# A GRU scan on one core: a quarter of the z product moved behind the turns of r*h, one filling unit moved behind the candidate in four steps of eight, and another order of three PSUM banks

## The chip, the core and the metric

The kernel runs on one core of one Trainium2 chip. The metric is the device time of one execution in microseconds. Three runs of the kernel before took 1352.71, 1353.44 and 1355.67 us; their median, 1353.44 us, is the time that the change is held against.

## The reference

A GRU runs over 128 steps for a batch of 64, with input and hidden width 512, all in float32. Every fourth step but the last also sends the new state through a dense layer with tanh, and that result is the state of the next step. The output is the input plus the states.

```python
def step(h, inp):
    x_t, prop = inp
    comb = jnp.concatenate([x_t, h], axis=-1)
    z = jax.nn.sigmoid(comb @ Wz + bz)
    r = jax.nn.sigmoid(comb @ Wr + br)
    comb2 = jnp.concatenate([x_t, r * h], axis=-1)
    h_cand = jnp.tanh(comb2 @ Wh + bh)
    h_new = (1.0 - z) * h + z * h_cand
    h_next = jnp.where(prop, jnp.tanh(h_new @ Wp + bp), h_new)
    return (h_next, h_new)
...
x = x + transpose(ys)
```

## The kernel before, in words

**Layout.** A state is a tile of 128 partitions and 256 columns: partitions 0 to 63 hold the batch with the first half of the hidden width, partitions 64 to 127 the batch with the second half. A matmul needs the state turned, so that the hidden width lies on the partitions. `turn` (line 206) does that for one half of the columns (c = 0 or 1): four bf16 transposes on TensorE, which move the float32 words as pairs of 16-bit words into PSUM, and one copy out of PSUM by VectorE or ScalarE (line 204), which joins the pairs.

**One product** of a gate is `h @ W` with the 512x512 lower half of a weight matrix: four quarters k of the contraction, each for the two halves of the output (`product`, line 197, and `products`, line 185). It appears in the profile as sixteen matmul records on line 188, so a quarter is four records. `ORDER` (line 201) takes both quarters that use column half c = 0 first, so that a product can start when half 0 of the turned state is there. The products of r and of the candidate go to the two halves of bank `rc`, those of z and of the dense layer to the two halves of bank `zp`. ScalarE seeds each slot beforehand with the x part and bias of that step (`seed`, line 393).

**The x parts** (`x @ W`, upper half of the weights) don't depend on the state. They are cut into small units that TensorE does between the products of the steps, where it would wait for the other engines. For the bulk of the steps the x parts of several steps are made with a scheme of seven products inside seven products, which saves multiplications and costs additions. `batch` (line 482) makes two of the outer products as fourteen units: two in bank `a`, then two each in banks `q`, `r` and `x` (`one_`, line 520), after which `end_1` (line 499) reads all four; then two each in `x`, `q`, `r` on top of what stands there (`two_`, line 521), after which `end_2` (line 511) reads `q` by ScalarE (line 514) and then `r`, `x`, `q` by VectorE (lines 515, 516 and 517, in this order). A unit is two logical matmuls and four records of 128x192.

**The order of the work** is written out by hand, engine by engine, in the order of the program text; each engine takes its own queue in order. `fill(n)` (line 401) issues the next n units. When a unit closes a batch half, its `end` isn't issued at once but at the next `read_out()` (line 411).

A step t (line 624 on) goes like this. TensorE: product r (line 660). ScalarE: two sigmoids of r (line 675); VectorE: two multiplications r*h (line 676). Meanwhile TensorE: product z, all four quarters (line 681). Then the two turns of r*h (line 685), copied by VectorE; then `fill(places[0])` (line 705); then the candidate's product (line 710), which needs the turned r*h. ScalarE has by then taken the sigmoid of z and of -z (lines 690 and 691), and VectorE `keep` = (1-z)*h (line 692). After the candidate: tanh on ScalarE (line 717), times z and plus `keep` on VectorE (lines 718 and 723), in two halves. TensorE meanwhile: `fill(5)` if `places[1]` is over 6, else `fill(4)` (line 727); turn of half 0 of the new state, copied by VectorE (line 731); `fill(1)` or `fill(2)` by the same rule (line 732); turn of half 1, copied by ScalarE (line 733); `fill(places[1] - 6)` (line 734). Then, in every fourth step, the dense layer's product, four units, its turns and two units (lines 740 to 751). Then the next step's product r.

`PLACES` (line 586) holds the counts for a cycle of eight steps, u = (t-3) mod 8. The last nine steps are called thin: they have their own table and already put half of the z product behind the turns of r*h, one quarter behind each turn.

Of the kernel before, what the change touches and what calls it, by code (L numbers as in the profile page):

```python
# [17 lines left out]
def kernel(  # L18
# [36 lines left out]
    K = D // P  # L55
# [4 lines left out]
    R, Z, H_ = range(3)  # L60
# [20 lines left out]
    wh = [const.tile([P, K, H], F32, name=f"wh_{i}") for i in range(3)]  # L81
# [49 lines left out]
    for g in (2, 3):  # L131
# [10 lines left out]
    slots = (rc[:, 0, :], zp[:, 0, :], rc[:, 1, :])  # L142
    slot_p = zp[:, 1, :]
    scratch = [ps_c.tile([P, 2 * N], F32, name=f"scratch_{n}") for n in "qrax"]
    q_ps, r_ps, a_ps, x_ps = (
        s[:, : 6 * P // 2].rearrange("p (m g u) -> p m g u", m=2, g=3) for s in scratch
    )
# [37 lines left out]
    def products(ps, lhs, rhs, start=False):  # L185

        for s in range(S):
            nc.tensor.matmul(  # L188
                ps[s * B : (s + 1) * B],
                lhsT=lhs,  # L190
                rhs=rhs(s),
                start=start,
                stop=True,
                skip_group_check=True,
            )

    def product(ps, lT, w, k, start=False):
        s0, c0 = divmod(k, C)
        products(ps, lT[:, c0, ts(s0, B)], lambda s: w[:, k, ts(s, N)], start)

    ORDER = [s * C + c for c in range(C) for s in range(S)]
# [4 lines left out]
    def turn(src, dst, c, name, eng):  # L206


        pt = turn_ps[c][:, :P].bitcast(BF16).rearrange("p (w n) -> p w n", w=2)
        for s in range(S):  # L210
            words = src[:, c * P + s * B : c * P + (s + 1) * B].bitcast(BF16)
            for w in range(2):
                nc.tensor.transpose(  # L213
                    pt[s * B : (s + 1) * B, w, :],
                    words.rearrange("p (n w) -> p w n", w=2)[:, w, :],
                    ident16,
                )
        copy(
            eng,
            dst[:, c, :].bitcast(U16).rearrange("p (n w) -> p n w", w=2),  # L220
            pt.bitcast(U16).rearrange("p w n -> p n w"),
        )

    def new_T(tag, name):
        return two.tile([P, C, P], F32, tag=tag, name=name)
# [71 lines left out]
    def factor(i, j):  # L297

        return {
            1: lambda: inner(i, 0, 0),  # L300
            2: lambda: inner(i, 1, 0),
            3: lambda: inner(i, 1, 1),
            4: lambda: tt[:, i - 1, 2],
            5: lambda: inner(i, 0, 1),
            6: lambda: tt[:, i - 1, 0],
            7: lambda: tt[:, i - 1, 1],
        }[j]()
# [57 lines left out]
    def lhs(g, i, j):  # L365

        if i in (1, 2):
            rows, s = (xT[g][:, 0, i - 1], xT[g][:, 1, i - 1]), lambda n: sx[g, 12][:, n, i - 1]
        elif i == 4:
            rows, s = (xT[g][:, 2, 1], xT[g][:, 3, 1]), lambda n: sx[g, 4][:, n]  # L370
        else:
            key, tab, n0 = {
                5: ("o12", 56, 0), 6: ("o12", 56, 1), 7: ("o34", 73, 0), 3: ("o34", 73, 1)
            }[i]
            o = sx[g, key][:, n0]
            rows, s = (o[:, 0], o[:, 1]), lambda n: sx[g, tab][:, n, n0]
        if j in (1, 2):
            return rows[0][:, ts(j - 1, B)]
        if j == 4:
            return rows[1][:, ts(1, B)]  # L380
        return s({5: 0, 6: 1, 7: 2, 3: 3}[j])
# [100 lines left out]
    def batch(n, ms):  # L482

        def region(ps, m):
            return ps[:, m].rearrange("p g u -> p (g u)")

        def unit(ps, m, j, start):
            g, i = ms[m]
            products(
                region(ps, m), lhs(g, i, j), lambda s: factor(i, j)[:, s], start and m == 0  # L490
            )

        def units(ps, j, start):
            return [lambda m=m: unit(ps, m, j, start) for m in range(len(ms))]

        def blocks():
            return MB[n].rearrange("p m b g (a u) -> p m b a g u", a=2)

        def end_1():
            MB[n] = mbp.tile([P, 2, 2, 3, P], F32, tag="mb", name=f"mb_{ms[0][0]}_{ms[0][1]}")  # L500
            for m, (g, i) in enumerate(ms):
                M[g, i] = MB[n][:, m]
            nm = len(ms)
            T2[n] = one.tile([P, 2, 3, P // 2], F32, tag="cx", name=f"cx_{ms[0][0]}_{ms[0][1]}")
            q1 = one.tile([P, 2, 3, P // 2], F32, tag="cq", name=f"cq_{ms[0][0]}_{ms[0][1]}")
            nc.scalar.copy(T2[n][:, :nm], x_ps[:, :nm])  # L506
            nc.scalar.copy(q1[:, :nm], q_ps[:, :nm])
            nc.vector.tensor_add(T2[n][:, :nm], r_ps[:, :nm], T2[n][:, :nm])  # L508
            nc.vector.tensor_add(blocks()[:, :nm, 0, 0], a_ps[:, :nm], q1[:, :nm])

        def end_2():
            q2 = one.tile([P, 2, 3, P // 2], F32, tag="cq", name=f"cq2_{ms[0][0]}_{ms[0][1]}")
            nm = len(ms)
            nc.scalar.copy(q2[:, :nm], q_ps[:, :nm])  # L514
            nc.vector.tensor_add(blocks()[:, :nm, 0, 1], r_ps[:, :nm], q2[:, :nm])  # L515
            nc.vector.tensor_add(blocks()[:, :nm, 1, 0], x_ps[:, :nm], q2[:, :nm])  # L516
            nc.vector.tensor_add(blocks()[:, :nm, 1, 1], q_ps[:, :nm], T2[n][:, :nm])  # L517

        free = units(a_ps, 2, True)
        one_ = units(q_ps, 1, True) + units(r_ps, 5, True) + units(x_ps, 7, True)  # L520
        two_ = units(x_ps, 4, False) + units(q_ps, 6, False) + units(r_ps, 3, False)
        seq = [(u, None) for u in free + one_ + two_]
        for n_units, end in ((4 * len(ms), end_1), (7 * len(ms), end_2)):
            seq[n_units - 1] = (seq[n_units - 1][0], end)
        return seq
# [4 lines left out]
    def batches(g):  # L530

        if g * Q4 >= T:
            return []
        ms = [(g, i) for i in (1, 2, 6, 5, 7, 3, 4)]
        if g + 1 < LAST:
            ms += [(g + 1, i) for i in (1, 6, 2, 5, 3, 7, 4)]
        return sum((batch((g, n), ms[2 * n : 2 * n + 2]) for n in range(7) if 2 * n < len(ms)), [])
# [43 lines left out]
    def outer_c21(g):  # L581
# [2 lines left out]


    PLACES = (
        (6, 8, 6), (2, 6), (6, 6), (2, 6), (6, 8, 6), (2, 6), (2, 6), (6, 8),
    )


# [14 lines left out]
    hT = new_T("hT", "hT_init")  # L605
# [18 lines left out]
    for t in range(T):  # L624
# [16 lines left out]
        thin = t >= T - 9  # L641
# [36 lines left out]
        join(0)  # L678


        for k in ORDER[: 2 if thin else K]:
            product(slots[Z], hT, wh[Z], k)
        rhT = new_T("rhT", f"rhT_{t}")
        for c in range(C):
            turn(rh, rhT, c, f"rhT_{t}", nc.vector)
            if thin:
                product(slots[Z], hT, wh[Z], ORDER[2 + c])
        z = two.tile([P, N], F32, tag="z", name=f"z_{t}")
        keep = two.tile([P, N], F32, tag="keep", name=f"keep_{t}")
        nc.scalar.activation(z, slots[Z], AF.Sigmoid)  # L690
# [38 lines left out]
        if not last:  # L729
            hT = new_T("hT", f"hT_{t}")  # L730
# [9 lines left out]
        if prop:  # L740
# [7 lines left out]
            hT = new_T("hT", f"hpT_{t}")  # L748
# [122 lines left out]
```

## Time and profile before

| what | value |
|---|---|
| median of three runs | 1353.44 us |
| the profiled execution: its time | 1353.16 us |
| its span, first to last instruction | 1351.3 us |
| what lies around the span | 1.9 us |
| TensorE matmuls busy | 1339.2 us, 15344 records |
| VectorE busy | 679.8 us |
| ScalarE busy | 628.2 us |
| GpSimd busy | 910.1 us |
| DMA traffic | 76.21 MB, 56 GB/s on average |
| TensorE clock granted | 0.997 of full speed |

How to read it: the span is that of one execution. "Busy" is the time in which an engine has at least one instruction under way. For matmuls the ends are modelled, so that a row of matmuls with small stalls between them can still show as busy without a break; the starts of instructions and the chain of work that ended last show more. In the timeline, equal instructions that follow each other are merged into one line, with their count; a bracket gives the idle time of the engine before it, and what is taken to have ended it. In the chain view, each line gives the start of a piece, its length and the engine and tile.

### The profile page before, as it was taken

The numbers are of one execution on the slowest core, as the hardware profiler recorded it, in microseconds if no ns is written. First come the engines' busy times: TensorE is split into PE (matmuls) and PEld (weight loads), VectorE is DVE, ScalarE is ACT, GpSimd is POOL, SyncE is SP. The second block draws the span as 40 slices with busy tenths as digits, with TensorE's granted clock in tenths as the row PEclk, the third lists the DMA queues.
The fourth block names the chain that finished last, engine by engine and source line by source line (L and its number), as shares of the span: only waits on it lengthen the run. The fifth ranks groups of instructions, "written<-read, shape, count | busy, mean of one in ns | idle before, by whom it ended". The sixth has DMA issues, their size and how long they took to land.

```text
span 1351.3 us, 37427 instructions
## 1 busy us (share of the span) xinstructions
PE 1339.2 (99%) x15344; PEld 1114.8 (82%) x15344; DVE 679.8 (50%) x1868; ACT 628.2 (46%) x1848; POOL 910.1 (67%) x1111
## 2 busy tenths in 40 slices
PE   9999999999999999999999999999999999999998
PEld 6878888888888888888888888888888888888765
DVE  3355555555555555554555555555555555555444
ACT  1234545444544544455445454545445444554433
POOL 3438676777767777676787767787677776767400
PEclk8999999999999999999999999999999999999999
DMA  9111223122321212313212231222213222131300
GB/s 280 22 33 33 64 48 79 33 49 48 64 64 33 64 42 55 64 33 73 52 35 64 56 73 33 49 48 64 64 33 64 48 49 64 33 73 39 102 17 17
DMA packets 114867, 76.21 MB, mean 56 GB/s; under 512 B 61700, under 2 KB 109956, under 8 KB 114696
## 3 DMA queue, kind: packets, MB, share of 16 engines
q1 hardware_dynamic: 113632, 72.04, 23.7%
q8 instruction: 121, 1.98, 0.6%
q10 hardware_dynamic: 1064, 1.78, 0.4%
q14 instruction: 50, 0.41, 0.1%
HBM read 42.34 MB, written 16.78 MB: 44 GB/s over the span
## 4 chain that ended last, share of the span: by engine, by line
PE 98%; DVE 1%; ACT 0%; issue 0%; POOL 0%; DVEq 0%; ACTq 0%; POOLq 0%
PE rc L188 34%; PE zp L188 20%; PE scratch_q L188 11%; PE scratch_x L188 11%; PE scratch_r L188 10%; PE scratch_a L188 6%; PE turn L213 5%; PE scratch_q L180 0%; PE zp L161 0%; ACT xT L204 0%; DVE rh L676 0%; PE rc L161 0%; DVE mb L516 0%; DVE mb L517 0%; DVE turn L718 0%
## 5 line engine op out<-in xcount | busy, mean ns | idle before, releaser
L188 PE MATMUL rc<-wh,rhT 128*64 128x256 f32 x2048 | 247.5, 381 | 0.0
L188 PEld LDWEIGHTS rc<-wh,rhT 128*64 128x64 f32 x2048 | 167.3, 137 | 45.2 <-ACT zp L691 9.3
L544 POOL TENSOR_TENSOR cp<-mb,mb 128x768 f32<-128x768 f32 x72 | 130.9, 1818 | 103.2 <-ACT rc L395 61.1
L188 PE MATMUL rc<-wh,hT 128*64 128x256 f32 x1536 | 186.6, 383 | 0.5
L188 PE MATMUL zp<-wh,hT 128*64 128x256 f32 x1536 | 186.9, 379 | 0.0
L803 POOL TENSOR_TENSOR xr<-xr,h 128x256 f32<-128x256 f32 x127 | 92.9, 732 | 115.2 <-DVE h L723 114.2
L204 DVE COPY rhT<-turn 128x256 uint16<-128x256 uint16 x256 | 97.6, 420 | 119.8 <-PE turn L213 118.8
L188 PEld LDWEIGHTS zp<-wh,hT 128*64 128x64 f32 x1536 | 130.4, 137 | 31.4
L718 DVE TENSOR_TENSOR turn<-turn,z 128x128 f32<-128x128 f32 x256 | 75.4, 295 | 148.9 <-ACT turn L717 148.8
L544 POOL TENSOR_TENSOR cp<-mb 128x768 f32<-128x768 f32 x44 | 80.0, 1818 | 103.6 <-ACT rc L395 102.4
L188 PEld LDWEIGHTS rc<-wh,hT 128*64 128x64 f32 x1536 | 123.0, 136 | 27.0 <-issue 1.3
L204 ACT COPY hT<-turn 128x256 uint16<-128x256 uint16 x127 | 47.3, 373 | 170.2 <-PE turn L213 113.6
L508 DVE TENSOR_TENSOR cx<-scratch_r,cx 128x384 f32<-128x384 f32 x102 | 56.7, 556 | 129.5 <-ACT cx L506 129.5
L675 ACT ACTIVATE turn<-rc 128x128 f32<-128x128 f32 x256 | 55.4, 261 | 141.3 <-issue 72.5
L717 ACT ACTIVATE turn<-rc 128x128 f32<-128x128 f32 x256 | 55.2, 260 | 131.5 <-PE rc L188 131.5
L544 POOL TENSOR_TENSOR mb<-mb,mb 128x768 f32<-128x768 f32 x58 | 105.7, 1822 | 12.5 <-DVE mb L517 12.5
L515 DVE TENSOR_TENSOR mb<-scratch_r,cq 128x384 f32<-128x384 f32 x102 | 56.7, 556 | 98.8 <-ACT cq L514 98.8
L395 ACT COPY rc<-cp 128x256 f32<-128x256 f32 x254 | 95.6, 376 | 13.2 <-PE rc L188 1.7
L274 ACT COPY xT<-xv 128x512 uint16<-128x512 uint16 x112 | 85.7, 765 | 0.0
L723 DVE TENSOR_TENSOR h<-turn,keep 128x128 f32<-128x128 f32 x254 | 74.1, 292 | 15.4
L690 ACT ACTIVATE z<-zp 128x256 f32<-128x256 f32 x128 | 49.2, 385 | 65.6 <-PE zp L188 60.8
L213 PEld LDWEIGHTS <-h 128*64 128x64 bf16 x1016 | 59.7, 110 | 22.2 <-DVE h L723 12.3
(156 smaller groups left out, 2981.2 us busy)
## 6 DMA issues: line engine op xcount, KB each, us to landing
xr<-in_x_dram SPq DMA_DIRECT2D x62, 256.0 KB, 4.2
out_dram<-xr SPq DMA_DIRECT2D x62, 256.0 KB, 3.4
xs<-in_x_dram SPq DMA_DIRECT2D x56, 256.0 KB, 4.2
wh<-in_L_cond_Wr_dram SPq DMA_DIRECT2D x2, 512.0 KB, 7.5
wh<-in_L_cond_Wz_dram SPq DMA_DIRECT2D x2, 512.0 KB, 6.6
wh<-in_L_cond_Wh_dram SPq DMA_DIRECT2D x2, 512.0 KB, 9.1
early<-in_x_dram SPq DMA_DIRECT2D x4, 256.0 KB, 12.2
wp<-in_L_cond_Wp_dram SPq DMA_DIRECT2D x1, 1024.0 KB
```

What stands on the lines that cost most here:

```text
L188: nc.tensor.matmul(ps[s * B : (s + 1) * B], lhsT=lhs, rhs=rhs(s), start=start, stop=True, skip_group_check=True,)
L204: (eng.copy if eng is nc.scalar else eng.tensor_copy)(dst, src)
L213: nc.tensor.transpose(pt[s * B : (s + 1) * B, w, :], words.rearrange("p (n w) -> p w n", w=2)[:, w, :], ident16,)
L274: nc.scalar.copy(xT[g][:, i].bitcast(U16).rearrange("p c (n w) -> p w c n", w=2), xv[g][:, i])
L395: nc.scalar.copy(cut(slots[i]), G[t][:, :, i, :])
L508: nc.vector.tensor_add(T2[n][:, :nm], r_ps[:, :nm], T2[n][:, :nm])
L515: nc.vector.tensor_add(blocks()[:, :nm, 0, 1], r_ps[:, :nm], q2[:, :nm])
L544: nc.gpsimd.tensor_add(dst, a, b)
L675: nc.scalar.activation(act_ps[c], slots[R][:, ts(c, P)], AF.Sigmoid)
L718: nc.vector.tensor_mul(pc, pc, z[:, ts(c, P)])
L723: nc.vector.tensor_add(h_new[:, ts(c, P)], pc, keep[:, ts(c, P)])
L803: nc.gpsimd.tensor_add(xr[g][:, j, :], xr[g][:, j, :], h_new)
```

## The change

Three things change, all in the order in which TensorE's instructions are issued; no instruction is added or taken away.

1. In all steps but the last nine, three quarters of the z product stand ahead of the turns of r*h, and the fourth follows both turns.
2. In the four steps of eight whose entry in `PLACES` was (2, 6), it is now (1, 7). By the rules of lines 705 and 727 to 734, one unit instead of two stands ahead of the candidate's product; behind it stand five units, the turn of half 0, one unit, the turn of half 1 and one unit, instead of four units, turn, two units, turn and none. The sum stays at eight units a step.
3. In the first half of a batch the banks are filled in the order r, x, q instead of q, r, x.

```diff
-        one_ = units(q_ps, 1, True) + units(r_ps, 5, True) + units(x_ps, 7, True)
+        one_ = units(r_ps, 5, True) + units(x_ps, 7, True) + units(q_ps, 1, True)
...
     PLACES = (
-        (6, 8, 6), (2, 6), (6, 6), (2, 6), (6, 8, 6), (2, 6), (2, 6), (6, 8),
+        (6, 8, 6), (1, 7), (6, 6), (1, 7), (6, 8, 6), (1, 7), (1, 7), (6, 8),
     )
...
-        for k in ORDER[: 2 if thin else K]:
+        for k in ORDER[: 2 if thin else 3]:
             product(slots[Z], hT, wh[Z], k)
         rhT = new_T("rhT", f"rhT_{t}")
         for c in range(C):
             turn(rh, rhT, c, f"rhT_{t}", nc.vector)
             if thin:
                 product(slots[Z], hT, wh[Z], ORDER[2 + c])
+        if not thin:
+            product(slots[Z], hT, wh[Z], ORDER[3])
         z = two.tile([P, N], F32, tag="z", name=f"z_{t}")
```

## The prediction

> **What bounds the kernel now.** I read the page first: TensorE's share of busy time, then the chain of work that ended last.
>
> ```profile
> PE 98%; DVE 1%; ACT 0%; issue 0%; POOL 0%; DVEq 0%; ACTq 0%; POOLq 0%
> ```
>
> The chain is TensorE almost throughout, and a table of windows gives 1062.00 us of matmul in the 1062 us from 118 to 1180: no idle time at all. That reading can't show small stalls, so I went to the chain in order of time, where each stage has its own length.
>
> ```profile
> 582.89 0.86 PE scratch_q L188 x8
> ...
> 607.65 1.79 PE rc L188 x16
> 609.44 0.65 PE scratch_q L188 x8
> 610.09 0.65 PE scratch_r L188 x8
> 610.74 0.15 PE turn L213 x4
> 610.89 0.65 PE scratch_x L188 x8
> 611.54 0.11 PE turn L213 x4
> 611.65 1.83 PE rc L188 x16
> 613.48 1.73 PE zp L188 x16
> ```
>
> Equal work takes unequal time. A product is 1.73 us (z, last line), but the candidate's took 1.79 and the r product of the next step 1.83; half a turn is 0.11, but one took 0.15; two units are 0.65, but those of bank q behind the dense layer took 0.86. The excess is stall. In this step, a (2, 6) one, it is 0.06 + 0.04 + 0.10 = 0.20 us. Steps with three units or more at each place have 1.73 and 0.11 throughout.
>
> Who is late is seen in the timeline (start, length, engine, line).
>
> ```profile
> 607.46 1.52 PEld L188 LDWEIGHTS rc<-wh,rhT 128*64 128x64 f32 x16 [0.16 <-ACT zp L691]
> ...
> 610.98 0.41 DVE L204 COPY hT<-turn 128x256 uint16<-128x256 uint16 x1
> ...
> 611.50 1.52 PEld L188 LDWEIGHTS rc<-wh,hT 128*64 128x64 f32 x16
> ```
>
> The weight load is named as waiting for ScalarE, but it needs the turned r*h: turns begin at 606.58, VectorE's first copy of them ends near 607.34. The r product of the next step waits in the same way: its copy ends at 611.39, its load starts 0.11 later, its first matmul at 611.54, 0.04 behind its load. The stall of bank q is VectorE's line 517:
>
> ```profile
> 582.28 0.55 DVE L517 TENSOR_TENSOR mb<-scratch_q,cx 128x384 f32<-128x384 f32 x1
> ...
> 582.88 0.20 PEld L188 LDWEIGHTS scratch_q<-tw,o 128*64 128x64 f32 x4 [0.44 <-DVE mb L517]
> ```
>
> **The Trainium skill.** "Perfetto Trace Analysis", section "Tensor Engine Instruction (MATMUL, LD_WEIGHTS)", says that a matmul's end is an estimate and its start is what is recorded; this trace agrees (busy without a break, yet 1.83 beside 1.73), so I use starts. "TensorE: Matmul & The Clock Gate", section "Step-by-step: what each phase is for", says that weight loads are pulled ahead of running matmuls while matmuls keep their order: here a load leads its matmul by 0.2 us in an unstalled stage (604.63 and 604.85 for a z product), and by 0.04 where it waited. So a late matmul delays all behind it; nothing overtakes. "PSUM — Partial Sum Buffer", section "PSUM bank collisions raise a hardware error", asks that reader and writer of a bank be kept apart by waits; that is the wait for line 517, and the order of the banks decides which reader it is.
>
> **Part 1, bank order.** In u = 0 the four units behind the dense layer begin a new half batch while VectorE still reads the old one: line 515 (bank r) runs from 581.34 to 581.90, 516 (x) to 582.36, 517 (q) to 582.83. Begun with r, TensorE could start at 581.95, before it is due at 582.70; x is due 0.65 later, q after the dense layer's turns. The stall goes: 0.86 - 0.65 = 0.21 us, 14 times from t = 11 on (the list of waits has 15 with t = 3), 2.9 us. At t = 3 VectorE is further behind: line 515 ends at 86.91 and 517 at 87.85, so r starts 0.94 earlier. In the other places the first half batch starts a product or more after line 517, and nothing changes. `end_1` reads x first and q second, and q is now the last written: ScalarE's copy of q waits, but the sigmoid that stands behind it needs a product r that ends 1.73 later. Cost nothing.
>
> **Part 2, z's last quarter behind the turns.** The product's own time doesn't change: 4 x 0.43. What it moves is the turns, 0.43 us earlier, and the risk is r*h being late.
>
> ```profile
> 613.28 1.93 PE L188 MATMUL zp<-wh,hT 128*64 128x256 f32 x16
> ...
> 613.86 0.49 DVE L676 TENSOR_TENSOR rh<-turn,h 128x128 f32<-128x128 f32 x2 [0.35 <-ACT turn L675]
> ...
> 614.80 0.47 PEld L213 LDWEIGHTS <-rh 128*64 128x64 bf16 x8
> ```
>
> The second r*h ends at 614.35. With three quarters the turn of half 0 is due at 613.28 + 12 x 0.108 = 614.58, half 1 at 614.69. From a VectorE end to the load that waits for it is 0.05 (610.53 to 610.58 at the turn of h), and 0.04 more to the matmul: ready at 614.44, 0.25 us of margin. I took the same difference in all steps from t = 11 to 118: 0.22 to 0.33, but for one at 0.09. No stall, and cost nothing. The thin steps, with only half of z ahead, have 0.17 for half a turn in the chain, 0.06 of stall: 0.43 us more cover is ample.
>
> At the start it isn't. In t = 0 to 3 turns of x stand ahead of z, ScalarE copies them ahead of the sigmoids, and the second r*h ends 1.50 us after z's first matmul (25.59 and 27.09): it is ready for a matmul at 1.58 where 1.41 is wanted, 0.17 x 4 = 0.7 us. In t = 4 and 5 the chain runs through ScalarE's copies and VectorE to r*h (turns at 94.73 and 105.30) and not through z at all; the quarter that is moved behind the turns loses its cover: 0.43 x 2 = 0.86.
>
> z ends 0.22 us later, behind the turns. ScalarE's two sigmoids, the copy of line 274 and the z seed then end near 608.65 in the step shown (today 608.43), with tanh due near 609.16; `keep` ends near 608.25. Margin 0.5 us; if it were gone, tanh, and behind it the state, would slip by as much. The z seed is also the last read of its x part, for which GpSimd waits before it overwrites; GpSimd is idle a third of the span. The queue of SP is untouched.
>
> **Part 3, (1, 7), with part 2.** Candidate: its load may start 0.88 us after the turns' first matmul (606.58, 607.46), its matmul at 0.92. Before, it was due at 0.22 + 0.65 = 0.87: late. Now at 0.22 + 0.43 + 0.33 = 0.98. Stall gone. Four steps of a cycle lose 0.06 each (0.05 in u = 1).
>
> Behind the candidate, counted from its end E (609.24): five units end at 1.63, over the 1.34 at which the new state's half 0 is ready, so the turn's 0.04 goes (u = 1 hadn't got it). VectorE's copy starts 0.35 after the turn (579.76, 580.11), at 1.98, free of the addition that ends at 1.82; it ends at 2.39, load 2.50, matmul 2.54. The r product is due at 1.63 + 0.11 + 0.33 + 0.11 + 0.33 = 2.51. So 0.03 is left, and about 0.02 inside the product, as stalled products have today (1.75 from first matmul to the next stage): 0.05 instead of 0.10 (0.07 in u = 1). The turn of half 1 comes at the same place as before; its copy has a unit more.
>
> Per cycle: candidate 0.23, turns 0.12, r product 0.05 + 0.05 + 0.05 + 0.02 = 0.17, together 0.52. Fourteen cycles: 7.3 us. A (6, 6) step keeps its 0.14.
>
> **Sum:** -7.3 - 2.9 - 0.9 + 0.7 + 0.9 = -9.5 us. The profiled execution took 1353.16 (span 1351.3 and 1.9 around it): 1343.7. It stands 0.3 below the median of the runs; against that, 1343.9 us. The unknown terms: the residue of the r product may be nothing (0.05 x 56 = 2.8 us faster) or the whole of today's tail may stay, which is rival (a); one more change between transposes and products a step isn't shown apart, and has a bound of 0.03, the excess that I find in mixed stages at the start (107 x 0.03 = 3.2 slower). A gain from it I exclude: the pieces already follow each other at full pace. I take nothing for it.
>
> **Rivals.** (a) The tail isn't mended: one unit between the half turns is too little to cover the copy, the r product is as late as before, and only bank q and the candidate's stall go: -3.2 - 2.9 + 0.7 = -5.4, 1348 us. For it: the margin is 0.03 on the wrong side already. Against: the sum above. (b) Slower: r*h comes late in every step, since z's three quarters no longer cover sigmoid and multiplication. It decides once the second r*h slips by more than 0.25 us, for example behind line 517 in VectorE's queue; each further 0.1 costs 10.7 us in 107 steps, so beyond 0.34 the change loses: with 0.45, 20 lost against 9.5, 1364 us. Against: half batches are read at the same places, and earlier relative to the r product, not later. (c) No change: what is saved in front of one wait is waited for in the next, since VectorE, ScalarE and TensorE form a loop; 1353. Against: steps with more filling show no stall, so the loop through the other engines is shorter than TensorE's work.
>
> **Chances.** Forecast (1340.5 to 1346.5) 0.74, (a) 0.14, (b) 0.07, (c) 0.05. A measurement of this kernel can tell about 0.2% from no change. Faster by more: 0.88; within: 0.05; slower: 0.07. The range adds (a) to the forecast's own: 1340.5 to 1348.5.
>
> **What would show it.** In the chain of the changed kernel: candidate 1.73, turn 0.11 and r product near 1.78 in the four steps; 0.65 for bank r behind the dense layer, and no wait for line 517; the turns of r*h 1.30 us after z's first matmul at 0.22. It is wrong if the r*h turns take longer than 0.22 in the bulk, or the r product stays at 1.83.

## The result, and the profile after

The changed kernel takes 1344.05 us (median of five runs, 1342.88 to 1345.45), against 1353.88 us for the kernel before, measured beside it. The ratio is 0.9928, with a 95% interval of 0.9916 to 0.9939: 9.8 us less. The forecast was 1343.9.

The page of the profiled execution has a span of 1341.0 us (before 1351.3), and TensorE is as full as it was:

```profile
PE 1329.3 (99%) x15344; PEld 1113.4 (83%) x15344; DVE 702.2 (52%) x1868; ACT 626.6 (47%) x1848; POOL 908.7 (68%) x1111
PE 99%; DVE 1%; issue 0%; ACT 0%; POOL 0%; DVEq 0%; POOLq 0%; ACTq 0%
```

The number of matmuls is the same, and the share of busy time too: neither shows where 10 us went. The chain in order of time does (start, length, piece). First the dense layer of a step with u = 0 and what follows it, then a (1, 7) step:

```profile
576.93 1.73 PE zp L188 x16
578.66 0.65 PE scratch_r L188 x8
579.31 0.65 PE scratch_x L188 x8
579.96 0.22 PE turn L213 x8
580.18 0.65 PE scratch_q L188 x8
```

```profile
600.53 1.29 PE zp L188 x12
601.83 0.22 PE turn L213 x8
602.05 0.43 PE zp L188 x4
602.48 0.33 PE scratch_a L188 x4
602.81 1.73 PE rc L188 x16
604.53 0.33 PE scratch_a L188 x4
604.86 0.65 PE scratch_r L188 x8
605.51 0.65 PE scratch_x L188 x8
606.16 0.11 PE turn L213 x4
606.27 0.33 PE scratch_q L188 x4
606.60 0.11 PE turn L213 x4
606.71 0.33 PE scratch_q L188 x4
607.04 1.79 PE rc L188 x16
```

The first units behind the dense layer take 0.65, not 0.86. The turns of r*h stand between three quarters of z (1.29) and the fourth (0.43) and take 0.22: they don't wait. The candidate is at 1.73 (it was 1.79), the turn of half 0 at 0.11 (0.15), and the next r product at 1.79 (1.83). Only that last one still has an excess, 0.06 us.

For the candidate a rival stands in the old profile itself, which names ScalarE's sigmoid of -z (line 691 before, 693 after) as what its weight load waited for. In the changed kernel the load starts before that sigmoid does, by 0.28 us here and in the other (1, 7) steps from t = 6 on, so it can't have been that:

```profile
602.52 1.56 PEld L188 LDWEIGHTS rc<-wh,rhT 128*64 128x64 f32 x16
...
602.80 0.38 ACT L693 ACTIVATE zp<-zp 128x256 f32<-128x256 f32 x1
```

For the r product the timeline shows the order of the work ahead of it:

```profile
604.34 0.52 PE L188 MATMUL scratch_a<-wx,xT 128*64 128x192 f32 x4
...
605.96 0.31 PE L213 MATMUL turn<-ident,h 128*64 128x128 bf16 x4
...
606.31 0.42 DVE L204 COPY hT<-turn 128x256 uint16<-128x256 uint16 x1 [0.16 <-PE turn L213]
...
606.85 1.52 PEld L188 LDWEIGHTS rc<-wh,hT 128*64 128x64 f32 x16 [0.16 <-issue]
606.88 1.95 PE L188 MATMUL rc<-wh,hT 128*64 128x256 f32 x16
```

The candidate's end, taken as the start of the unit behind it, is 604.34. The turn of half 0 comes 1.62 after it, VectorE's copy 0.35 after that and ends at 606.73, the weight load starts 0.12 later and its matmul 0.03 behind it: 2.54 after the candidate, as worked out in the prediction. The profile names no engine for this wait ("issue"); that it is VectorE's copy is read from the times here, and tried below by giving the copy to ScalarE.

To see where in the run the time went, I compare the start of each step's first sigmoid (line 675) in the two traces. By stretch:

| stretch | forecast | trace, us |
|---|---|---|
| before step 0 | 0 | -0.57 |
| steps 0 to 5 | +0.6 (-0.94 + 0.70 + 0.86) | +0.12 |
| steps 6 to 10 | in the cycles | -0.42 |
| steps 11 to 114, thirteen cycles | -0.73 each | -0.689 each, -8.96 |
| steps 115 to 118 | in the cycles | -0.28 |
| thin steps | 0 | -0.27 |

The sum is the span's -10.4. Leave out what lies before step 0 and in the thin steps, where the change does nothing to the program's work, and -9.5 remains, which is the forecast's sum. Its parts are not the forecast's: the three rows of the cycles make -9.66, where fourteen cycles were to bring -10.2, and the start makes +0.12, where +0.6 was forecast.

### The profile page after: what moved, and what is told of

Read it like the earlier page. It is cut to its first block, busy times and chain, and to the rows that moved or that the text cites. A ratio compares the mean times of both kernels' runs of the same rounds, so it can differ in the third digit from the quotient of the medians.

```text
span 1341.0 us, 37605 instructions
## 1 busy us (share of the span) xinstructions
PE 1329.3 (99%) x15344; PEld 1113.4 (83%) x15344; DVE 702.2 (52%) x1868; ACT 626.6 (47%) x1848; POOL 908.7 (68%) x1111
## 4 chain that ended last, share of the span: by engine, by line
PE 99%; DVE 1%; issue 0%; ACT 0%; POOL 0%; DVEq 0%; POOLq 0%; ACTq 0%
PE rc L188 34%; PE zp L188 20%; PE scratch_q L188 11%; PE scratch_x L188 11%; PE scratch_r L188 10%; PE scratch_a L188 6%; PE turn L213 5%; PE scratch_q L180 0%; PE rc L161 0%; ACT xT L204 0%; PE zp L161 0%; DVE rh L676 0%; DVE turn L720 0%; DVE bias L169 0%; DVE h L725 0%
## 5 line engine op out<-in xcount | busy, mean ns | idle before, releaser
L188 PE MATMUL zp<-wh,hT 128*64 128x256 f32 x1536 | 204.5, 379 | 0.0
L188 PEld LDWEIGHTS rc<-wh,hT 128*64 128x64 f32 x1536 | 121.9, 137 | 36.5 <-issue 10.4
L188 PEld LDWEIGHTS zp<-wh,hT 128*64 128x64 f32 x1536 | 119.1, 137 | 24.5
L213 PEld LDWEIGHTS <-h 128*64 128x64 bf16 x1016 | 68.2, 110 | 12.9 <-DVE h L725 4.6
```

The costliest lines, as they stand in the source:

```text
L188: nc.tensor.matmul(ps[s * B : (s + 1) * B], lhsT=lhs, rhs=rhs(s), start=start, stop=True, skip_group_check=True,)
L213: nc.tensor.transpose(pt[s * B : (s + 1) * B, w, :], words.rearrange("p (n w) -> p w n", w=2)[:, w, :], ident16,)
```

## The experiments

Two theories were to be told apart: the forecast's (three separate stalls, each with a length that follows from the order of TensorE's work and the time that the other engines need) and the rivals: (a) the tail stays as it was, (b) r*h comes late without z's fourth quarter, (c) what is saved at one wait is lost at the next. The first four kernels were measured beside the kernel before at 1353.19 us, the next four at 1353.44.

### The bank order alone

```diff
-        one_ = units(q_ps, 1, True) + units(r_ps, 5, True) + units(x_ps, 7, True)
+        one_ = units(r_ps, 5, True) + units(x_ps, 7, True) + units(q_ps, 1, True)
```

> The kernel before with the order of the banks alone (r, x, q). Forecast's theory: only the wait for VectorE's last read of bank q behind the dense layer goes, 0.21 us in 14 cycles and 0.94 at t = 3: 3.8 us less, about 1350.1 against 1353.9; in the chain, the units of bank r behind the dense layer take 0.65 per two, and everything else keeps its stalls (candidate 1.79, r product 1.83). Rival (what is saved at one wait is lost at the next): no change.

Measured: 1349.77 us, ratio 0.9971 (0.9960 to 0.9982), 3.4 us less. From step to step the trace gives 0.206 us per cycle and 0.85 at t = 3. In the chain, two units of bank r behind the dense layer take 0.65, and a (2, 6) step keeps its stalls:

```profile
583.07 0.65 PE scratch_r L188 x8
...
607.62 1.79 PE rc L188 x16
...
610.71 0.15 PE turn L213 x4
...
611.63 1.83 PE rc L188 x16
```

The wait for line 517 was on the path, and what it cost wasn't taken back anywhere.

### z's last quarter behind the turns, alone

```diff
-        for k in ORDER[: 2 if thin else K]:
+        for k in ORDER[: 2 if thin else 3]:
...
+        if not thin:
+            product(slots[Z], hT, wh[Z], ORDER[3])
```

> The kernel before with z's last quarter behind the turns alone; places and banks as before. Theory: the candidate's stall goes (0.23 a cycle, 3.2 us), the start loses about 1.2 us, the tail behind the candidate keeps its 0.14 a step: 2.0 us less, about 1351.9. Rival (b), r*h late without z's fourth quarter ahead of it: slower, by 1 us for each 0.01 us that a turn of r*h waits.

Measured: 1351.38 us, ratio 0.9985 (0.9978 to 0.9991), 1.8 us less. In the trace a cycle gains 0.244 and the first six steps lose 1.34. The chain of a (2, 6) step shows both the stall that goes and those that stay:

```profile
608.36 0.22 PE turn L213 x8
608.59 0.43 PE zp L188 x4
609.02 0.65 PE scratch_a L188 x8
609.67 1.73 PE rc L188 x16
611.40 0.65 PE scratch_q L188 x8
612.05 0.65 PE scratch_r L188 x8
612.70 0.15 PE turn L213 x4
612.85 0.65 PE scratch_x L188 x8
613.50 0.11 PE turn L213 x4
613.61 1.83 PE rc L188 x16
```

The turns of r*h at 0.22 speak against (b); the unchanged 0.15 and 1.83 say that z's quarter doesn't mend the tail.

### The places (1, 7), alone

```diff
-        (6, 8, 6), (2, 6), (6, 6), (2, 6), (6, 8, 6), (2, 6), (2, 6), (6, 8),
+        (6, 8, 6), (1, 7), (6, 6), (1, 7), (6, 8, 6), (1, 7), (1, 7), (6, 8),
```

> The kernel before with the places (1, 7) alone; the whole z product ahead of the turns. Theory: the turned r*h is ready for the candidate 0.92 us after the turns begin, and only 0.22 + 0.33 = 0.55 of work stands there: 0.37 of stall in four steps of eight instead of 0.06, while the tail gains 0.29 a cycle: 1.0 us a cycle more, 14 us in all, about 1368. Rival (c), the loop through the other engines takes the difference up: no change, 1354. Rival (a), the tail isn't mended by this split: 1372.

Measured: 1368.48 us, ratio 1.0108 (1.0093 to 1.0124), 15.3 us more; 1.075 us per cycle in the trace, where 1.0 was expected. In the chain of this kernel the candidate's product behind one unit, and the tail behind it, are

```profile
614.16 1.95 PE rc L188 x16
...
617.73 0.11 PE turn L213 x4
...
618.61 1.79 PE rc L188 x16
```

The 1.95 is a part of the stall. By starts, the unit ahead of the candidate and the wait behind it take 0.68 to 0.70 in this trace, where a unit takes 0.33: 0.35 to 0.37 of wait, as expected. The tail is mended just as in the changed kernel. So (c) is out: a stall of this size isn't taken up by anything. And parts 2 and 3 belong together: alone they give -1.8 and +15.3, together -5.6 (next kernel). The unit that is taken from in front of the candidate may only go because z's quarter has come there.

### Both of these, with the old bank order

The changed kernel with the bank order of the kernel before:

```diff
-        one_ = units(r_ps, 5, True) + units(x_ps, 7, True) + units(q_ps, 1, True)
+        one_ = units(q_ps, 1, True) + units(r_ps, 5, True) + units(x_ps, 7, True)
```

> The changed kernel with the old order of the banks (q, r, x). Theory: the parts add up, and this loses just what the bank order alone gains: 3.8 us over the changed kernel, about 1347.9. Rival: the other two parts already bring line 517 in time, and the bank order is worth nothing here: 1344.

Measured: 1347.56 us, ratio 0.9954 (0.9941 to 0.9966), 5.6 us less than before. With the bank order's 3.4 that makes 9.0, against 9.8 for all of it: within the intervals they add. In the traces a cycle gains 0.477 here and 0.206 there, 0.683 together, against 0.689 for all of it. The chain has the old 0.86 behind the dense layer in this kernel too; the other parts don't bring line 517 in time.

### Two quarters of z behind the turns

```diff
-        for k in ORDER[: 2 if thin else 3]:
+        for k in ORDER[:2]:
...
-            product(slots[Z], hT, wh[Z], ORDER[3])
+            for k in ORDER[2:]:
+                product(slots[Z], hT, wh[Z], k)
```

> The changed kernel with two quarters of z, not one, behind the turns of r*h in all steps (the thin ones put both behind both turns as well). It tests the margin of 0.25 us. Theory: the turns are due 0.43 us earlier, the second r*h misses them by 0.16 to 0.18 on average in 107 steps, 18 us, and by 0.43 more in the six first steps, 2.6 us: about 20 us over the changed kernel, 1364. Rival (b) in its strict form, the margin is only the lead that a weight load needs, 0.05: each step loses 0.37, 1384. Rival: the two halves of r*h are turned apart, and the first covers the second: no more than 1350.

Measured: 1363.84 us, ratio 1.0078 (1.0064 to 1.0092), 10.4 us more than before and some 20 more than the changed kernel. In the chain:

```profile
603.20 0.86 PE zp L188 x8
604.06 0.37 PE turn L213 x8
604.43 0.87 PE zp L188 x8
605.29 0.65 PE scratch_r L188 x8
```

The turns take 0.37 instead of 0.22. By starts, z's first half and the turns take 1.26 in this step (603.00 to 604.26) where 1.09 is the work: 0.17 of stall. Over the steps 11 to 118 it is 0.16 on average, and only some 0.10 in two of the eight steps of a cycle (u = 1 and 5), where r*h is ready sooner. From step 11 to 115 the trace gives 0.145 per step more than the changed kernel, 15 us; the first six steps give 4.3. So the sum was right, its parts were not: the bulk less, the start more than the expected 18 and 2.6, and that they balance is luck. The margin of the forecast is real, and it ends where it was said to end: in the bulk three quarters is free, two is not. The strict form of (b), a margin of 0.05, would have made 40, and the first half of r*h doesn't cover the second.

### The copies of the new state exchanged

The changed kernel, with half 0 copied by ScalarE and half 1 by VectorE:

```diff
-            turn(h, hT, 0, f"hT_{t}", nc.vector)
+            turn(h, hT, 0, f"hT_{t}", nc.vector if thin else nc.scalar)
...
-            turn(h, hT, 1, f"hT_{t}", nc.scalar)
+            turn(h, hT, 1, f"hT_{t}", nc.scalar if thin else nc.vector)
```

> The changed kernel with the engines of the two copies of the new state exchanged, but for the thin steps: half 0 by ScalarE, half 1 by VectorE. Theory: what is left of the r product's stall (0.06 in four steps of a cycle) is VectorE's copy of half 0; ScalarE's takes 0.37 instead of 0.42 and its engine has been idle for half a microsecond, and the r product then needs one wait less: the 0.06 goes in 56 steps, and in the (6, 6) steps the r product's 0.07, where VectorE's addition stands in front of its copy: 3.4 + 1.0 us less than the changed kernel, about 1339.6. Rival: the residue is the weight load's own start after transposes, whoever copies: 1344. Rival: VectorE's copy of half 1 comes late for the r product's second half: over 1344.

Measured: 1339.24 us, ratio 0.9896 (0.9883 to 0.9910), 14.2 us less than before, so 4.4 less than the changed kernel. Chain and timeline:

```profile
605.24 0.11 PE turn L213 x4
605.35 0.33 PE scratch_q L188 x4
605.68 0.11 PE turn L213 x4
605.79 0.33 PE scratch_q L188 x4
606.12 1.73 PE rc L188 x16
```

```profile
605.40 0.37 ACT L204 COPY hT<-turn 128x256 uint16<-128x256 uint16 x1 [0.84 <-PE turn L213]
...
605.82 0.49 PEld L188 LDWEIGHTS rc<-wh,hT 128*64 128x64 f32 x6
605.84 0.42 DVE L204 COPY hT<-turn 128x256 uint16<-128x256 uint16 x1 [0.60 <-PE turn L213]
605.95 0.60 PE L188 MATMUL rc<-wh,hT 128*64 128x256 f32 x4
```

The r product is at 1.73. A cycle gains 0.35 more than in the changed kernel (1.036 against 0.689). The copy is 0.05 shorter, and the load starts 0.05 behind its end instead of 0.12; in all the load now leads its matmul by 0.13. So the residue was the copy of half 0 and the wait behind it, not a start-up of the product. How much of it is the shorter copy and how much the shorter wait wasn't tried apart.

### The start as before, and both together

The changed kernel with all of z ahead of the turns in the first six steps; and the same on top of the exchanged copies.

```diff
-        for k in ORDER[: 2 if thin else 3]:
+        for k in ORDER[: 2 if thin else K if t < 6 else 3]:
...
-        if not thin:
+        if not thin and t >= 6:
             product(slots[Z], hT, wh[Z], ORDER[3])
```

> The changed kernel with the whole z product ahead of the turns in the first six steps, as before. Theory: the start gets back what it lost, 0.12 in each of t = 0 to 3 and 0.44 in t = 4 and in t = 5 by the trace: 1.3 us less, about 1342.8, and the step that ends the start, t = 6, begins 1.3 us earlier. Rival: t = 4 and 5 wait for VectorE anyway, the stall only changes its place: no change.

> The exchange of the copies and the old start together in the changed kernel. Theory: both gains add, 4.4 + 1.3 us less than the changed kernel, about 1338.4. Rival: the exchange gains nothing, 1342.8.

Measured: 1342.61 us, ratio 0.9924 (0.9911 to 0.9936), and 1337.69 us, ratio 0.9884 (0.9869 to 0.9899). Against the changed kernel's 0.9928 the first can't be told by the time alone; in the trace, steps 0 to 5 take 1.04 us less, where 1.3 was expected: 0.47 in t = 0 to 3, as expected, and 0.57 in t = 4 and 5 instead of 0.88 (the reason is in the next section). The second is 15.8 us less than before, the fastest version here, where the sum of the expected gains was 15.5; in its trace a cycle gains 1.044 (1.036 with the copies alone), and the first six steps take 1.02 less than there.

## Why the prediction was right, step by step

- **Bank order.** Forecast 0.21 a cycle and 0.94 at t = 3; alone it gave 0.206 and 0.85.
- **z's quarter.** "No stall" in the bulk: the turns of r*h take 0.22 in the changed chain, and by the same reckoning the margin is 0.23 to 0.32 us (the old trace promised 0.22 to 0.33), but for one step, t = 14, where it falls about 0.01 short and the turns take 0.005 longer. Two quarters behind the turns show that the margin has an end.
- **z later by 0.22.** Two sigmoids, copy, seed, tanh: in the step shown, ScalarE is idle for 0.49 ahead of tanh (604.63), against the forecast 0.5. GpSimd's waits didn't reach the chain.
- **(1, 7).** Candidate and turn as forecast; the r product keeps 0.06 instead of 0.05. A cycle gains 0.483 from parts 2 and 3 (0.689 less 0.206; 0.477 in the kernel with the old bank order), forecast 0.52.
- **The mis-sized term: the start.** Forecast +0.70 for t = 0 to 3 and +0.86 for 4 and 5; with the bank order taken out, steps 0 to 5 lost 0.95 instead of 1.56. In steps 0 to 3 it is 0.12 each, not 0.17. In t = 4 and 5 the quarter alone cost 0.87 in its own experiment, as forecast; with the places (1, 7) it cost 0.50. The difference is part 3, which was put at nothing there: t = 4 is a (1, 7) step, and the unit that now stands behind the turn of half 1 fills a wait of the turn of x behind it for ScalarE's copy (0.53 before, 0.20 after). With all of z ahead of the turns that move gains only 0.07 in t = 4 and 5 (the places alone, and the old start), since the candidate then has too little cover, as in every (1, 7) step without z's quarter.
- **By luck.** The start cost 0.5 less than forecast and the cycles gained 0.54 less (9.66, not 10.2). The two misses cancel, so that the sum of -9.5 is met far more closely than its parts. The span's other 0.84, 0.57 before step 0 and 0.27 in the thin steps, no part of the forecast covers.

## What to carry to other kernels

Where an engine is busy without a gap, compare stages of equal work in the chain of the trace: the excess over the shortest is stall, and the cure here was a reordering, not less work. Work out for each wait when its data is ready, counted from a common event, and when it is due: the difference says how much filling work has to stand there, and any beyond that is free to go where another wait falls short. Two moves can be right together and wrong alone, so cost the cover of each wait after all moves, not after one.

## What the runs showed of the hardware that was not expected

- The start of step 0 varied from 0.58 us earlier to 2.09 us later than in the kernel before, over nine executions whose instructions up to there do the same work. Differences smaller than that are read from step to step, not from spans.
- VectorE's busy time rose by 22.4 us (679.8 to 702.2) with the same 1868 instructions. `keep` now waits for ScalarE in all 128 steps (64.1 us) where it waited in nine (6.3); queued instructions of VectorE overlap in the timeline, and those that wait one by one don't. It is at most half of it: with z's quarter alone, where `keep` waits just as long, VectorE is busy for 691.0 us, and with the places alone, where it waits in nine steps, for 687.9. Busy shares of two kernels that differ by a few per cent don't show more or less work here.
- In the (1, 7) steps the weight load of the r product started 0.05 us after the end of the copy that it waited for when that copy was ScalarE's, and 0.12 after it when it was VectorE's. In the second case the trace has a separate wait of 0.05 us in front of the load (606.77), since the load itself also waits for ScalarE.
- In the traces with the new bank order, the last nine steps are 0.13 to 0.30 us shorter, in those with the old order they differ by 0.02 at most: the first sigmoid of t = 124 starts 2.32 us behind the first matmul of its product in the kernel before, and 2.04 with the new order. The cause stays open.
- At t = 39 one addition of VectorE (line 725) stands idle for 0.46 us ahead of its start, behind its own engine's last instruction, in the changed kernel and in three others (z's quarter alone, the old bank order, two quarters); in the kernel with the old start it doesn't. The turns of the new state wait for it, and that cycle gains 0.59 where the others gain 0.69 to 0.70. The cause stays open.
